# Cross attention in Strassen form: the fourth product moved in front of the next energy, and y's split ahead of gx's

## The chip, the cores and the metric

The kernel runs on one core of one Trainium2 chip. Its five engines work side by side: TensorE (PE) multiplies matrices into eight PSUM banks, VectorE (DVE), ScalarE (ACT) and GpSimd (POOL) work element by element, and SyncE (SP) issues transfers. The kernel fixes the order of the instructions on each engine; between engines it orders them by semaphores. Time is in microseconds (us) of device time for one execution of the whole program, lower is better.

## The reference

`x` and `y` (ctx) have shape 32 x 256 x 1024 in float32: 32 batches, 256 channels, 1024 positions. For each batch:

```python
x_q = w_qk @ y            # transposed: N x C
x_k = w_qk @ x
x_v = w_v @ x + b_v
energy = x_q.T @ x_k                               # N x N, 1024 x 1024
attention = softmax(energy, axis=-1)               # rows
attention = attention / (1e-7 + attention.sum(axis=1))   # columns
x_r = x_v @ attention
out = x + relu(w_t @ (x - x_r) + b_t)
```

The weights are 256 x 256. The column sums need all rows of the softmax, so the second half of a batch can't start before the whole energy has been exponentiated.

## The kernel before, in words

**Algebra.** The two uses of w_qk are folded into one matrix G, so that energy = y.T (G x). w_t and w_v are folded too, so that the output is w_t x minus (w_t w_v x) times the attention. Three products of a batch are done by a 2 x 2 block scheme of Winograd's kind with seven block products P1 to P7 in place of eight: `Keys` (gx = G x, names `pg`), `Values` (u, names `pu`) and `Attention` (the output, names `po`). Each has three PSUM banks, `one`, `two` and `three`. `one` takes P1, then P6 is added, then P7, then P4; between these additions a copy is read out of it: P1 (`p1s`), P1+P6 (`w`), with P7 (`c22`), with P4 (`c21`). `two` takes P5 (`p5s`), then P3 (`c12`); `three` takes P2 (`c11`). So a product that goes into `one` has to wait until the value before it has been read. `Attention`'s P-products consist of one part on x (`xpart`) and four on the attention tiles (`epart`, tiles 0 to 3). All seven are float32 products of 128 x 512, two matmul instructions each.

**Energy.** gx and y are each split into three parts in a faster matmul type (`Split`, tiles `gf` and `yf`): the high part, the lower part, and a mixed part. `parts(i)` writes all three on ScalarE for half i of the channels (3 instructions); `lower(i)` adds the original to the lower part by an accumulating transfer that GpSimd issues; `mixed(i)` adds the finished lower part to the mixed part by another one, which can be issued only after `lower(i)` has landed. The energy of row block n (8 of them) and column half h is six matmuls: two on the high parts, two on the lower, two on the mixed ones, so that the sixth of a row block's first half is the first to need the mixed part of half 1. `gather` copies one sum on ScalarE (`es`) and adds the other on VectorE while taking the row minimum; `exp` is ScalarE, `share` adds the row to the column sums (`acc`) on VectorE.

**Order of a batch.** The order is written out by hand: the class `InOrder` chains every instruction of an engine behind the one before it. A batch goes: energy rows 0 to 7; then `Keys` and the first part of `Values` of the next batch while VectorE finishes the column sums (`columns`, `inverse`); then the attention (`Attention.run`). In `run`, VectorE scales the exponentials (`normal`, 16 instructions) and makes the sums t1 to t4 of attention blocks (`mix`, two instructions each). t3 is written over t1 and t4 over t2, so t3 must wait until P5 has read t1, and t4 until P6 has read t2. The last product of the attention, P4 (`end`, `before.end()`, 5 products), with its read-out `c21`, stands in the next batch's energy, behind row block 0.

**Other queues.** GpSimd issues the eight accumulating transfers of the split, then the small copy `behind` that reads t4 (so that the following does not run beside the mixes), then the sums of the value blocks (`factors`: two additions to `ut`, four to `us`), then three accumulating transfers (`xsteps`) for the sums of x. SP issues the loads of y (two batches ahead), the four stores of the output blocks, two loads for the sums of x (`summed`) and the load of x (`load(b + 1)`).

**Buffers.** The eight PSUM banks are handed out in turn. `us`, `yf`, `gf`, `acc` and the attention tiles `e` and `et` have one buffer each; the output temporaries `z` have two.

Of the kernel before, what the change touches and what calls it, by code (L numbers as in the profile page):

```python
# [12 lines left out]
ALU = mybir.AluOpType  # L13
# [4 lines left out]
def kernel(  # L18
# [25 lines left out]
    KC = C // P  # L44
# [3 lines left out]
    HT = NT // 2  # L48
# [29 lines left out]
    pe, dve, act, pool = (InOrder(g) for g in (nc.tensor, nc.vector, nc.scalar, nc.gpsimd))  # L78
# [6 lines left out]
    def load(b, pieces=1):  # L85
        to = xp.tile([P, KC, N], F32, tag="x", name=f"x_{b}")
        from_ = x[b].rearrange("(k p) n -> p k n", p=P)
        W = KC // pieces
        for j in range(pieces):
            nc.sync.dma_start(to[:, ts(j, W)], from_[:, ts(j, W)])  # L90
        loaded[b] = to
# [43 lines left out]
    behind = const.tile([P, 1], F32, name="behind")  # L135
# [70 lines left out]
    def temp(tag, name):  # L206
        return cp.tile([P, MB], F32, tag=tag, name=name)
# [8 lines left out]
    def summed(b):  # L216

        s = up.tile([P, 4, MB], F32, tag="xs", name=f"xs_{b}")
        t1, t3, t4, t2 = (s[:, j] for j in range(4))
        to = loaded[b]  # L220
        b11, b12 = to[:, 0, ts(0, MB)], to[:, 0, ts(1, MB)]
        b21, b22 = to[:, 1, ts(0, MB)], to[:, 1, ts(1, MB)]
        if b == 0:
            pool.tensor_tensor(t1, b11, b12, ALU.add)
            pool.tensor_tensor(t2, b22, t1, ALU.add)
            pool.tensor_tensor(t3, b12, b22, ALU.add)
            pool.tensor_tensor(t4, b21, t2, ALU.add)
            steps = []
        else:
            q = quarters(x[b])  # L230
            nc.sync.dma_start(s[:, :2], q[:, 0, 1:2, :].to_broadcast([P, 2, MB]))
            nc.sync.dma_start(s[:, 2:], q[:, 1])
            steps = [
                lambda: accumulate(s[:, :2], corners(x[b])),
                lambda: accumulate(s[:, 2:], s[:, 0:1].to_broadcast([P, 2, MB])),
                lambda: accumulate(t4, q[:, 1, 1]),
            ]
        return (b11, b21, b22, t4, t1, t2, t3), steps
# [211 lines left out]
    class Attention(Seven):  # L450
# [76 lines left out]
        def run(self, u, before=None, between=None):  # L527


            self.normal(0, 0)  # L530
            self.normal(1, 0)
            for j in range(HT // 2):
                self.normal(0, 1, j)
                self.mix(self.t1, self.b11, self.b12, ALU.add, j)
            if u:
                u.c22()
            self.normal(1, 1)
            self.mix(self.t2, self.t1, self.b22, ALU.subtract)
            self.epart(self.one, 1)
            self.p1s = self.biased(self.one, "p1s", bt[:, 0, :])  # L540
            if u:
                between.parts(1)
                between.lower(1)
                between.mixed(1)
            self.epart(self.three, 2)
            self.epart(self.two, 5)
            self.p5s = self.biased(self.two, "p5s", bt[:, 1, :])
            self.xpart(self.one, 6, True)
            if u:
                u.p4()  # L550
                u.c21()
                u.c11()
                u.c12()
            self.c11()
            self.put()
            self.xpart(self.two, 3, True)
            self.epart(self.two, 3, (0, 1) if u else (0,))
            self.epart(self.one, 6)
            self.w = self.biased(self.one, "w", nbt[:, 0, :])
            self.mix(self.t3, self.b12, self.b22, ALU.subtract)  # L560
            if before:
                before.combine(1, 1, before.p5s, before.p7s, ALU.subtract)
                before.put()
                before.c21()
            self.mix(self.t4, self.b21, self.t2, ALU.subtract)
            self.epart(self.two, 3, (2,) if u else (1, 2))
            if u:
                self.epart(self.two, 3, (3,))
                self.c12()

        def end(self):
            self.xpart(self.one, 4, True)
# [20 lines left out]
    def columns(b):  # L593

        dve.tensor_reduce(
            parts[:, :, 0],
            acc.rearrange("p (j r) -> p j r", r=G32),
            AX.X,
            ALU.add,
            apply_transpose=True,  # L600
        )
# [22 lines left out]
    q = Queries(0)  # L624
# [4 lines left out]
    g = Keys(0, xr)  # L629
# [26 lines left out]
    u = Values(0, xr)  # L656
# [10 lines left out]
    before = None  # L667
    for b in range(B):
        more = b + 1 < B
        rows = []  # L670

        for n in range(NT):
            now = Energy(b, n, q.to, g.split.to)
            rows.append(now)
            now.products(0)
            if n == 0:
                e = ep.tile([P, NT, N], F32, tag="e", name=f"e_{b}")
                acc = one.tile([P, N], F32, tag="acc", name=f"acc_{b}")
            now.gather(0)
            now.products(1)  # L680
            now.gather(1)
            if n == 0:
                if b == 0:
                    u.p4()
                    u.c21()
                    xsteps[1]()
                    xsteps[2]()
                elif more:
                    before.end()
                    before.c21()  # L690
                    load(b + 1)
                if before is not None:

                    pool.tensor_copy(behind, before.t4[:, HT - 1, :1])
                if more:
                    ur, usteps = u.factors()
                    for step in usteps:
                        step()
                if more and b > 0:
                    xn, xsteps = summed(b + 1)  # L700
            if n > 0:
                rows[n - 1].exp()
            if n > 1:
                rows[n - 2].share()
            if more and b > 0 and n in (2, 4, 6):
                xsteps[n // 2 - 1]()

        if more:
            q = Queries(b + 1)
            for i in range(KC):  # L710
                q.load(i, nc.sync.dma_start)
            g = Keys(b + 1, xn)
            g.p1()
            rows[-1].exp()
            rows[-2].share()
            g.p5()
            g.p2()
            g.c11()
            rows[-1].share()
            g.p6()  # L720
            columns(b)
            g.p3()
            g.c12()
            g.p7()
            g.c22()
            un = Values(b + 1, xn)
            un.p1()
            un.p5()
            un.p2()
            un.p6()  # L730
        else:
            before.xpart(before.one, 7, True)
            rows[-1].exp()
            rows[-2].share()
            before.epart(before.one, 7)
            ur, usteps = u.factors()
            now = Attention(b, xr, ur)
            now.begin()
            rows[-1].share()
            columns(b)  # L740
            for step in usteps:
                step()
            before.p7s = temp("w", "p7s")
            act.copy(before.p7s, before.one)
        rc = inverse(b)
        if more:
            q.parts(0)
            q.lower(0)
            un.p3()
            g.p4()  # L750
            g.c21()
            un.p7()
            for i in range(KC):
                g.split.parts(i)
                g.split.lower(i)
            q.mixed(0)
            for i in range(KC):
                g.split.mixed(i)

        if more:  # L760
            now = Attention(b, xr, ur)
            now.begin()
            now.run(un, between=q)
            if b + 2 < B:
                now.xpart(now.one, 7, True)
                now.epart(now.one, 7)
                now.c22()
                now.put()
            now.put()
            before = now  # L770
            xr, u = xn, un
        else:
            before.end()
            now.run(None, before)
            now.finish()
# [30 lines left out]
```

## Time and profile before

| what | value |
|---|---|
| median of 3 runs | 2247.34 us (2243.19 to 2255.17) |
| the profiled execution | 2252.05 us, span 2250.2 us |
| TensorE / VectorE / ScalarE / GpSimd busy | 95% / 83% / 52% / 30% |
| mean granted TensorE clock | 0.973 |
| from one energy's start to the next, typical batch | 69.1 us (1006.61 to 1075.68) |
| of that, from the energy's first matmul to its restart behind P4 | 11.3 us (1006.61 to 1017.91) |

An instruction's line shows the start, the length, the engine, the operation, the tiles written and read (out<-in) and, in brackets, how long the engine was idle before it and what ended that. `L73` is the line of the helper that records every instruction, so tiles are told apart by their names: `pe` energy, `pg` gx, `pu` u, `po` output, `yfr` and `gfr` the unsplit rows. A stage's line gives its borders, its length, the busy time of PE, PE's weight loads, DVE, ACT and POOL, the granted clock (1.00 is full speed), the busy share of the DMA engines and their GB/s. Matmuls overlap their neighbours a little, so distances between starts are safer than the lengths shown.

### The profile page before, as it was taken

To read this page: it belongs to the slowest core of one execution; us is meant where nothing else is said; L and a number is where in the kernel's file an instruction comes from. 1 tells how busy PE (TensorE), PEld (TensorE's weight loads), DVE (VectorE), ACT (ScalarE), POOL (GpSimd) and SP (SyncE) were. 2 spreads that over 40 slices of the span, in tenths; PEclk is the share of its full clock that TensorE was granted. 3 is DMA by queue.
4 is the path that set the end of the run, shared out by engine and by line. 5 is a ranking of instruction groups with operands and counts; after the bars stand their busy time and mean duration, and the time that the engine had idled before them with its cause. 6 is when DMAs were issued, how large, how long until landed. Compare 5 with 4: busy or idle time off the path is not lost.

```text
span 2250.2 us, 23462 instructions
## 1 busy us (share of the span) xinstructions
PE 2132.7 (95%) x7586; PEld 1316.0 (58%) x7586; DVE 1875.9 (83%) x3024; ACT 1180.5 (52%) x1802; POOL 667.0 (30%) x582
## 2 busy tenths in 40 slices
PE   6999999999999999999999999999999999999998
PEld 4566555665556665556655566655666555665554
DVE  1988889877898888898788988888887789888888
ACT  4564545654456545556544565454664445654552
POOL 2333332223322333322233223333132332223321
PEclk7999999999999999999999999999999999999999
DMA  8455765646656567666476565675664756556650
GB/s 201 94 128 130 173 150 122 149 113 159 156 120 150 121 147 168 151 125 143 115 164 150 123 144 120 155 168 132 137 138 117 173 134 137 139 122 161 159 98 28
DMA packets 108954, 310.33 MB, mean 138 GB/s; under 512 B 10785, under 2 KB 11553, under 8 KB 108833
## 3 DMA queue, kind: packets, MB, share of 16 engines
q0 software_dynamic: 58192, 174.87, 42.4%
q1 hardware_dynamic: 50496, 133.85, 17.7%
q8 instruction: 60, 0.98, 0.2%
q14 instruction: 62, 0.50, 0.1%
q10 hardware_dynamic: 144, 0.13, 0.0%
HBM read 124.78 MB, written 33.55 MB: 70 GB/s over the span
## 4 chain that ended last, share of the span: by engine, by line
PE 72%; DMA 10%; issue 7%; ACT 6%; DVE 5%; POOL 0%; DVEq 0%; ACTq 0%; POOLq 0%
PE pe L73 30%; PE po L73 30%; PE pu L73 8%; DMA yf<-yf 6%; PE pg L73 4%; DVE e L73 3%; DMA yf<-yfr 2%; ACT e L73 2%; DMA gf<-gfr 1%; ACT gf L73 1%; ACT ow L73 1%; ACT es L73 1%; ACT yf L73 1%; ACT gp5s L73 1%; DVE acc L73 0%
## 5 line engine op out<-in xcount | busy, mean ns | idle before, releaser
L73 PE MATMUL pe<-gf,yf 128*128 128x512 f32 x3072 | 770.5, 410 | 87.9 <-DMA yf<-yf 78.2
L73 PEld LDWEIGHTS pe<-gf,yf 128*128 128x128 f32 x3072 | 591.0, 193 | 250.4 <-issue 109.4
L73 ACT ACTIVATE es<-pe 128x512 f32<-128x512 f32 x512 | 303.9, 594 | 465.4 <-PE pe L73 465.3
L73 PE MATMUL po<-et,us 128*128 128x512 f32 x768 | 350.3, 597 | 1.2 <-DVE et L73 1.2
L73 DVE SCALAR_TENSOR_TENSOR e<-e,ri,rc 128x512 f32<-128x512 f32 x512 | 347.4, 746 | 1.1
L73 DVE SCALAR_TENSOR_TENSOR acc<-e,ri,acc 128x1024 f32<-128x1024 f32 x224 | 289.9, 1294 | 8.0
L73 ACT ACTIVATE e<-e,nm 128x1024 f32<-128x1024 f32 x256 | 292.7, 1143 | 6.7 <-DVE nm L73 3.8
L73 DVE CUSTOM_DVE_ANT_0 e<-pe,es,nm 128x512 f32<-128x512 f32 x256 | 192.3, 751 | 81.2 <-ACT es L73 49.4
L73 PEld LDWEIGHTS po<-et,us 128*128 128x128 f32 x768 | 143.2, 190 | 192.9 <-issue 154.1
L73 PE MATMUL po<-e,ut 128*128 128x512 f32 x512 | 225.0, 592 | 1.0 <-DVE e L73 1.0
L73 DVE CUSTOM_DVE_ANT_0 e<-pe,es 128x512 f32<-128x512 f32 x256 | 175.6, 686 | 48.2 <-ACT es L73 32.0
L73 DVE SCALAR_TENSOR_TENSOR z<-z,x 128x512 f32<-128x512 f32 x96 | 214.6, 2260 | 1.2
L73 POOL DMA_DIRECT2D yf<-yfr x64 | 65.5, 1023 | 451.6 <-ACT yf L73 451.6
L73 PEld LDWEIGHTS po<-e,ut 128*128 128x128 f32 x512 | 97.2, 190 | 123.8 <-issue 107.9
L73 POOL TENSOR_TENSOR ut<-ut,bu 128x1024 f32<-128x1024 f32 x64 | 160.0, 2666 | 0.0
L73 POOL DMA_DIRECT2D yf<-yf x64 | 66.2, 1034 | 316.4 <-issue 267.5
L73 DVE TENSOR_TENSOR et<-e 128x1024 f32<-128x1024 f32 x128 | 153.7, 1222 | 5.1 <-DVE e L73 0.9
L73 ACT ACTIVATE yf<-yf 128x1024 fp32r<-128x1024 f32 x128 | 128.3, 1049 | 2.0
L73 ACT ACTIVATE gf<-gf 128x1024 fp32r<-128x1024 f32 x128 | 128.2, 1049 | 2.0
L73 POOL DMA_DIRECT2D xs<-in_x_dram x62 | 66.3, 1070 | 205.4 <-DMA xs<-xs 129.4
L73 PE MATMUL po<-e,us 128*128 128x512 f32 x256 | 120.5, 592 | 0.0
L73 PE MATMUL po<-et,ut 128*128 128x512 f32 x256 | 119.5, 610 | 0.0
(106 smaller groups left out, 2614.7 us busy)
## 6 DMA issues: line engine op xcount, KB each, us to landing
yfr<-in_ctx_dram SPq DMA_DIRECT2D x64, 512.0 KB, 6.4
yf<-yfr POOLq DMA_DIRECT2D x64, 512.0 KB, 6.1
gf<-gfr POOLq DMA_DIRECT2D x64, 512.0 KB, 5.8
yf<-yf POOLq DMA_DIRECT2D x64, 512.0 KB, 8.0
gf<-gf POOLq DMA_DIRECT2D x64, 512.0 KB, 9.4
out_dram<-z SPq DMA_DIRECT2D x128, 256.0 KB, 2.4
x<-in_x_dram SPq DMA_DIRECT2D x31, 1024.0 KB, 6.7
xs<-in_x_dram SPq DMA_DIRECT2D x62, 512.0 KB, 4.9
```

The costliest lines, as they stand in the source:

```text
L73: self.last = getattr(self.engine, name)(*args, **kwargs)
```

## The change

- P4 and its read-out leave the energy. A new `close()` at the attention's end holds P7, the last tile of P3, c22, P4, c12 and c21, so the energy of the next batch runs through all its rows without another product in between. In `run`, P3's tiles stand as 0, (P6), 1 and 2, (P7), 3.
- The split of y is issued in front of that of gx on ScalarE and on GpSimd: y's two halves first, lower and mixed, then gx's. What stands behind P1's copy in `run` is now the second half of gx (`between`) in place of the second half of y.
- GpSimd's `behind` and the sums of the values (`factors`) are written at the end of the attention of the same batch, in place of row block 0 of the next energy.
- The mix t3 stands directly behind t2 on VectorE, in front of u's c11 and c12 and of the output's c11.
- gx's P5 and its copy stand in front of the last row's exp.

```diff
             if u:
-                between.parts(1)
-                between.lower(1)
-                between.mixed(1)
+                between()
@@ run
                 u.c21()
+                self.mix(self.t3, self.b12, self.b22, ALU.subtract)
                 u.c11()
                 u.c12()
             self.c11()
             self.put()
             self.xpart(self.two, 3, True)
-            self.epart(self.two, 3, (0, 1) if u else (0,))
+            self.epart(self.two, 3, (0,))
             self.epart(self.one, 6)
             self.w = self.biased(self.one, "w", nbt[:, 0, :])
-            self.mix(self.t3, self.b12, self.b22, ALU.subtract)
             if before:
+                self.mix(self.t3, self.b12, self.b22, ALU.subtract)
...
             self.mix(self.t4, self.b21, self.t2, ALU.subtract)
-            self.epart(self.two, 3, (2,) if u else (1, 2))
-            if u:
-                self.epart(self.two, 3, (3,))
-                self.c12()
+            self.epart(self.two, 3, (1, 2))
+
+        def close(self):
+
+            self.xpart(self.one, 7, True)
+            self.epart(self.one, 7)
+            self.epart(self.two, 3, (3,))
+            self.c22()
+            self.put()
+            self.end()
+            self.c12()
+            self.put()
+            self.c21()
@@ energy, row block 0
                 elif more:
-                    before.end()
-                    before.c21()
                     load(b + 1)
-                if before is not None:
-
-                    pool.tensor_copy(behind, before.t4[:, HT - 1, :1])
-                if more:
+                if b == 0:
                     ur, usteps = u.factors()
                     for step in usteps:
                         step()
@@ behind the energy
             g.p1()
+            g.p5()
             rows[-1].exp()
             rows[-2].share()
-            g.p5()
...
             un.p7()
-            for i in range(KC):
-                g.split.parts(i)
-                g.split.lower(i)
+            q.parts(1)
+            q.lower(1)
             q.mixed(0)
-            for i in range(KC):
-                g.split.mixed(i)
+            g.split.parts(0)
+            q.mixed(1)
+            g.split.lower(0)
+
+            def between():
+                g.split.parts(1)
+                g.split.lower(1)
+                g.split.mixed(0)
+                g.split.mixed(1)
+
             now = Attention(b, xr, ur)
             now.begin()
-            now.run(un, between=q)
+            now.run(un, between=between)
+            pool.tensor_copy(behind, now.t4[:, HT - 1, :1])
             if b + 2 < B:
-                now.xpart(now.one, 7, True)
-                now.epart(now.one, 7)
-                now.c22()
+                now.close()
+                ur, usteps = un.factors()
+                for step in usteps:
+                    step()
+            else:
+                now.epart(now.two, 3, (3,))
+                now.c12()
                 now.put()
-            now.put()
```

## The prediction

> **What bounds the kernel now.** I read the page first, then the chain and the waits, then TensorE, GpSimd and VectorE in order of time in one typical batch (about 1006 us).
>
> From the page:
>
> ```profile
> span 2250.2 us, 23462 instructions
> PE 2132.7 (95%) x7586; PEld 1316.0 (58%) x7586; DVE 1875.9 (83%) x3024; ACT 1180.5 (52%) x1802; POOL 667.0 (30%) x582
> ```
>
> TensorE fills the span; VectorE, at 83%, is second. So the time is TensorE's work plus the places where it stops or runs slowly. The waits (total us, times, longest):
>
> ```profile
> PE pe L73 <- DMA yf<-yf: 78.2, 31, 3.7
> DVE z L73 <- ACT z L73: 103.6, 30, 5.1
> PE pg L73 <- ACT gp5s L73: 10.1, 31, 1.8
> PEld po L73 <- DVE et L73: 31.4, 63, 1.4
> ```
>
> TensorE has one wait of weight: once a batch, 2.5 us in the mean, for the transfer that forms y's third part. TensorE there, in order of time:
>
> ```profile
> 1003.58 3.60 PE L73 MATMUL po<-et,us 128*128 128x512 f32 x8
> 1006.61 1.72 PE L73 MATMUL pe<-gf,yf 128*128 128x512 f32 x5
> 1010.61 2.34 PE L73 MATMUL pe<-gf,yf 128*128 128x512 f32 x7 [2.27 <-DMA yf<-yf]
> 1012.75 1.91 PE L73 MATMUL po<-xs,wtT 128*128 128x512 f32 x2
> 1014.45 4.02 PE L73 MATMUL po<-et,ut 128*128 128x512 f32 x8
> 1017.91 19.63 PE L73 MATMUL pe<-gf,yf 128*128 128x512 f32 x84
> ```
>
> P7 ends, row 0 of the energy starts, its sixth matmul waits, then come seven matmuls, P4 (the two po lines) and the other 84 energy matmuls. The lines after the wait are slow: P4 takes 5.16 us (1012.75 to 1017.91), where the five equal products of P7 take 4.30 (1002.72 to about 1007.02). The stages say why (PEclk is the third figure from the end):
>
> ```profile
> 1010.60:1018.30 7.70, 7.69 (x18) 4.05 (x18) 4.71 (x6) 0.60 (x1) 6.75 (x5) 0.78 0.46 145
> 1018.30:1037.40 19.10, 19.10 (x86) 15.79 (x85) 14.94 (x35) 14.79 (x27) 3.33 (x3) 1.00 0.63 151
> ```
>
> A second price is thus paid after the wait, in granted clock. I read the two marks, first energy matmul and restart behind P4, in all 30 batches that have both. From restart to the next start it is 57.7 to 58.1 us nearly everywhere. From start to restart it is 9.09 to 13.88, mean 11.17. All that varies, and all that is lost, lies in that second stretch. Its work is 12 matmuls of 0.227 (82 take 18.61 in the chain) = 2.73, and P4's 4.30: 7.03. So 4.14 us a batch are lost, 2.5 to the wait and 1.6 to the clock.
>
> Why the transfer is late, GpSimd in order of time:
>
> ```profile
> 980.70 0.87 POOL L73 DMA_DIRECT2D yf<-yfr  x1 [12.73 <-ACT yf L73]
> 993.99 0.86 POOL L73 DMA_DIRECT2D gf<-gf  x1 [3.61 <-DMA gf<-gfr]
> 994.52 1.20 POOL L73 DMA_DIRECT2D yf<-yfr  x1
> 1006.01 0.86 POOL L73 DMA_DIRECT2D yf<-yf  x1 [10.28 <-issue]
> 1006.69 5.01 POOL L73 TENSOR_TENSOR ut<-ut,bu 128x1024 f32<-128x1024 f32 x2
> ```
>
> Eight accumulating transfers (two tensors, two halves, lower and mixed) go through one queue. With the issue-to-landing times of the DMA view, seven land at 985.9, 989.3, 993.5, 997.2, 1000.1, 1002.6 and 1005.5: 3.3 us apart in the mean, 2.5 to 4.2. The eighth, y's last, can be issued only when the seventh has landed (1006.01), with nothing else in the queue, and lands at 1010.6.
>
> **The change, part by part.**
>
> *P4 in front of the energy, per batch.* Five products of 0.86 move from behind row 0 to in front of it: no work is added. The same place in the new order, counted from this batch: P6 starts one product earlier, P7 ends at 1006.16, the last P3 product at 1007.02, P4 at 1011.3 plus a new wait. The new wait: P4 writes the bank that c22 reads on VectorE. The last batch already has this order at its end:
>
> ```profile
> 2240.74 1.02 PE L73 MATMUL po<-e,us 128*128 128x512 f32 x2
> 2241.68 1.13 PE L73 MATMUL po<-xs,wtT 128*128 128x512 f32 x2
> ```
>
> One P3 product (0.86) covers c22 (0.69, from 2240.94); P4 starts 0.08 late and its first product takes 0.11 longer. I take 0.2; ends 0.1 and 0.6 (0.54 is the longest wait of its kind on VectorE in that stretch). The energy starts at 1011.5.
>
> *y's forms ahead of gx's.* New GpSimd order: y lower 0 and 1, y mixed 0 and 1, then gx the same way. ScalarE's last three forms stay in the slot behind P1's copy, only now they are gx's. No transfer stands alone at the end now, since a mixed half has another half between it and its lower one. Eight landings, 3.3 apart from 985.9, end at 1008.9. The first matmul that needs the last one is the energy's sixth, at 1011.5 + 5 x 0.227 = 1012.6. Margin 3.7 us, so the wait goes to nothing. Bounds by the spacing rows: at 2.5 the last lands at 1003.4, at 4.2 at 1015.3, 2.7 late. I take the mean, since it is the same queue, with the same two y loads beside it.
>
> *The clock.* Half-speed stretches stand behind these waits; waits of 0.27 us (gx's P6 on its copy) have none behind them, the stage at 1018 to 1075 reads 1.00. So I take the 1.6 as gone; ends 0 and 1.6. The Trainium skill says otherwise: TensorE: Matmul & The Clock Gate, section "HAM oscillation — how this bites in real kernels", gives the rule that only idle gaps above about 3.4 us cost clock. By it a gap of 2.27 would not, and the 1.6 would stay, 2174 in all; the 0.78 above speaks against the rule.
>
> *GpSimd's sums at the attention's end.* Two adds to ut and four to us, 10.8 us (1006.69 to 1017.51), now start behind t4 (VectorE ends it at 1003.9), not behind y's last DMA: 1004.2 to 1015.0. They hold VectorE's adds of two SBUF tiles: a z add takes 0.69 alone, and with the first two sums beside it
>
> ```profile
> 998.72 0.69 DVE L73 SCALAR_TENSOR_TENSOR z<-z,x 128x512 f32<-128x512 f32 x1
> 1007.82 6.12 DVE L73 SCALAR_TENSOR_TENSOR z<-z,x 128x512 f32<-128x512 f32 x2
> 1019.23 0.69 DVE L73 TENSOR_TENSOR z<-z,x 128x512 f32<-128x512 f32 x1 [3.75 <-ACT z L73]
> ```
>
> that is, each is held until an idle moment of GpSimd. New: c22's put ends at 9.8 (ut's sums end 1009.2, and 0.55), c12's at 11.4, P4's z add, the third line above, is now held as well, to 1015.6. Behind it on VectorE stands the energy's first reduction, so at 4.1 us after the energy's start. TensorE needs that bank again with row 2, 28 x 0.227 = 6.4 after the start, so the reduction may start until 5.6. Rows 0 and 1 have no sum over rows, so VectorE catches up. Cost 0, cover 1.5 us; past that, each us costs 30 a run. The 3.75 wait for P4's z (103.6 in all) goes, worth nothing to TensorE. Next in GpSimd's queue is xs's first accumulate: at 1020.07 it waited 2.56 for TensorE, not for the sums, so it keeps its place behind the restart. P4's ScalarE pass now stands in front of row 0's first copy: it waits for P4 (1011.5) and for c22's store out of the same buffer (issued after 1009.8, 2.0 to 2.5 to land, so 1012.2) and ends at 1012.9; the copy, ready at 1012.6, is wanted by VectorE only at 1015.6. On SP, P4's store and the next x load follow the z add as before: x now about 2.1 us after the restart, 2.4 before. The two xs loads go in between the stores, no later.
>
> *Mix t3 behind t2* (2 x 1.2 us): it overwrites t1, which P5 has read by 993.3; t3 now starts at 996.8. The adds it passes (u's c11, c12, the output's c11 and put) come 2.35 later and feed only stores, bank releases and the sums, which start behind t4 anyway; t4 still ends at 1003.9. Cost 0, hidden under P6; without the cover 2.35.
>
> *gx's P5 ahead of the last exp*: removes the 0.27 of TensorE (10.1 / 31). But VectorE's t1 comes just in time for P5 (the 31.4 of weight loads on et, 0.5 each), so TensorE would only wait there. I take 0; ends 0 and -8 us in all. The exp comes 0.5 later; VectorE reads its sum 2 us after it.
>
> *The sum.* Per batch 11.17 - (2.73 + 4.30 + 0.2) = 3.94 saved, x 30 = 118. The last energy (no P4) waits 3.48 now; its last transfer comes some 3 us sooner: 3. Together 121. The profiled execution took 2252.05 (span 2250.2), 4.7 above the median 2247.34 of the three runs; the difference goes on the median: 2247 - 121 = 2126.
>
> **The rivals.**
>
> *The clock stays low* for another reason than the wait: 30 x 1.6 come back, 2174. For it: some batches with a 1.9 us wait show no loss, so the tie is not exact. Against: every stretch without the wait runs at 1.00.
>
> *VectorE late.* If the held z adds end 1 to 2 us past the cover, or c22's wait costs its upper end, 12 to 60 come back: 2138 to 2186. For it: single z adds took up to 5.7 us. Against: sums now start before the adds, so less of them is left to wait for.
>
> *The forms are later still, and it is slower.* Place: the energy's sixth matmul, now waiting for gx's last transfer, with the half clock behind it. The stretch is 7.23 + W + 1.6 and equals 11.17 at W = 2.3, a landing at 1014.9, a spacing of 4.1. At 4.6, the time of a transfer alone (1006.01 to 1010.6), it lands at 1018.1, W = 5.5: 30 x 3.2 = 95 more, about 2342. For it: one spacing of 4.2. Against: six had a mean of 3.3.
>
> *No change in effect*: the wait only changes its tensor and costs the same; 2236 to 2258 (0.5% is what a measurement of this kernel can tell). It needs a landing at 1014.7 to 1015.2, a narrow window.
>
> **How the numbers follow.** Forecast 0.70 (2106 to 2140: the gx wait's 8, and 12 for scatter, below; c22's upper end above), clock 0.07, VectorE 0.13, no change 0.04, slower 0.06. The first three are faster: 0.90, 0.04, 0.06. The range from 2106 to 2186 takes in the first three, less some tails.
>
> **What would show it.** Right: no TensorE wait for yf or gf of over 0.3 us past the first batch; granted clock near 0.99 over the run; start to restart gone, 64.7 to 65 us from energy to energy; y's last transfer before gx's first. Wrong: "PE pe <- DMA gf<-gf" at about 2 us a batch; VectorE's first reduction over 5.6 us after the energy's start with TensorE waiting for it; half clock behind the c22 wait.

## The result, and the profile after

The changed kernel takes 2131.1 us (median of 4, 2130.4 to 2133.0) against 2247.6 before: 0.948 of it, interval 0.9453 to 0.9506. The profiled execution has a span of 2128.9 us and a mean granted clock of 0.994 (before 0.973). The forecast was 2126, range 2106 to 2186.

From the page of the changed kernel:

```profile
span 2128.9 us, 23494 instructions
PE 2087.1 (98%) x7586; PEld 1290.6 (61%) x7586; DVE 1812.7 (85%) x3024; ACT 1179.7 (55%) x1802; POOL 681.3 (32%) x582
```

TensorE's 7586 instructions are as many as before, but their busy time is 46 us less: no work went, they no longer run at half clock. The rest of the 121 us of span is waiting. From its waits (total us, times, longest):

```profile
DVE z L73 <- ACT z L73: 51.2, 30, 2.5
PEld po L73 <- DVE et L73: 45.0, 62, 1.4
PE po L73 <- DVE et L73: 11.5, 33, 0.5
PE pe L73 <- DMA gf<-gf: 10.9, 3, 5.4
```

The line of 78.2 us for y's transfer is gone. What is left on a transfer is three waits, two of them in the first batch and one of 0.93 at the last energy. One line has grown from 1.2 us to 11.5: TensorE waits for VectorE's `et`, now once a batch. TensorE from P7 into the next energy, in order of time:

```profile
954.63 3.60 PE L73 MATMUL po<-et,us 128*128 128x512 f32 x8
958.07 1.02 PE L73 MATMUL po<-e,us 128*128 128x512 f32 x2
959.07 1.12 PE L73 MATMUL po<-xs,wtT 128*128 128x512 f32 x2
960.03 3.60 PE L73 MATMUL po<-et,ut 128*128 128x512 f32 x8
963.06 20.33 PE L73 MATMUL pe<-gf,yf 128*128 128x512 f32 x87
```

The first line is P7, the second the last P3 product, then P4 and the energy in one piece. P4 starts 0.14 late (959.07, not 958.93) and its first product takes 0.10 longer: that is the wait for c22, 0.24 in all. From one energy's start to the next it is 65.0 us from the third energy up to the last but one.

GpSimd in the same batch:

```profile
932.15 0.87 POOL L73 DMA_DIRECT2D yf<-yfr  x1 [15.38 <-ACT yf L73]
941.37 0.86 POOL L73 DMA_DIRECT2D yf<-yf  x1 [2.97 <-ACT gf L73]
951.71 0.86 POOL L73 DMA_DIRECT2D gf<-gf  x1 [7.72 <-DMA gf<-gfr]
954.46 0.86 POOL L73 DMA_DIRECT2D gf<-gf  x1 [1.89 <-DMA gf<-gfr]
956.07 4.66 POOL L73 TENSOR_TENSOR ut<-ut,bu 128x1024 f32<-128x1024 f32 x2
```

The last form is issued at 954.46 and lands 5.3 later, at 959.8; the matmul that needs it comes at about 964.6. Over 30 batches it lands 4.2 us ahead in the mean. VectorE, where the sums on GpSimd hold its adds:

```profile
959.04 2.23 DVE L73 SCALAR_TENSOR_TENSOR z<-z,x 128x512 f32<-128x512 f32 x1
961.91 1.04 DVE L73 SCALAR_TENSOR_TENSOR z<-z,x 128x512 f32<-128x512 f32 x1
964.68 1.21 DVE L73 TENSOR_TENSOR z<-z,x 128x512 f32<-128x512 f32 x1 [1.72 <-ACT z L73]
965.81 0.68 DVE L73 CUSTOM_DVE_ANT_0 e<-pe,es 128x512 f32<-128x512 f32 x1
```

All three z adds are held (0.69 alone), and the energy's first reduction starts at 965.81, 2.3 us after the energy's start (963.5, when P4's last product is out).

### The profile page after: what moved, and what is told of

Same layout as the page of the kernel before. It is cut to its first block, busy times and chain, and to the rows that moved or that the text cites. A ratio compares the mean times of both kernels' runs of the same rounds, so it can differ in the third digit from the quotient of the medians.

```text
span 2128.9 us, 23494 instructions
## 1 busy us (share of the span) xinstructions
PE 2087.1 (98%) x7586; PEld 1290.6 (61%) x7586; DVE 1812.7 (85%) x3024; ACT 1179.7 (55%) x1802; POOL 681.3 (32%) x582
## 4 chain that ended last, share of the span: by engine, by line
PE 61%; DVE 29%; issue 4%; ACT 1%; DMA 1%; DVEq 0%; POOL 0%; ACTq 0%; POOLq 0%
PE pe L73 31%; PE po L73 28%; DVE e L73 14%; DVE acc L73 4%; DVE et L73 4%; DVE gfr L73 3%; DVE rc L73 2%; DVE sc L73 1%; PE pu L73 1%; DVE parts L73 1%; ACT es L73 1%; DVE ri L73 0%; DMA gf<-gfr 0%; PE pg L73 0%; DMA gf<-gf 0%
## 5 line engine op out<-in xcount | busy, mean ns | idle before, releaser
L73 PE MATMUL pe<-gf,yf 128*128 128x512 f32 x3072 | 718.7, 394 | 10.9 <-DMA gf<-gf 10.9
L73 PEld LDWEIGHTS pe<-gf,yf 128*128 128x128 f32 x3072 | 578.0, 188 | 145.7 <-issue 27.3
L73 PE MATMUL po<-et,us 128*128 128x512 f32 x768 | 353.9, 597 | 11.5 <-DVE et L73 11.5
L73 POOL DMA_DIRECT2D yf<-yfr x64 | 55.0, 860 | 533.0 <-ACT yf L73 518.6
L73 ACT ACTIVATE z<-po,bt 128x512 f32<-128x512 f32 x31 | 21.4, 689 | 337.1 <-DMA out_dram<-z 234.5
L73 POOL TENSOR_TENSOR ut<-ut,bu 128x1024 f32<-128x1024 f32 x64 | 153.5, 2473 | 0.0
L73 POOL DMA_DIRECT2D gf<-gf x64 | 54.8, 856 | 306.3 <-DMA gf<-gfr 262.8
L73 DVE SCALAR_TENSOR_TENSOR z<-z,x 128x512 f32<-128x512 f32 x96 | 132.2, 1377 | 3.3
L73 PE MATMUL po<-e,us 128*128 128x512 f32 x256 | 125.3, 592 | 0.0
L73 POOL DMA_DIRECT2D xs<-xs x31 | 37.2, 1201 | 248.4 <-DMA xs<-in_x_dram 240.9
```

The lines of the kernel that those rows point to most:

```text
L73: self.last = getattr(self.engine, name)(*args, **kwargs)
```

## Experiments

All kernels start from the changed one unless it is said otherwise; `...` in an edit stands for lines left out. "Energy to energy" is the time from one energy's first matmul to the next one's. The runs were spread over several chips, on which the median of the kernel before was 2243.6 to 2248.6 us.

### One part at a time

**The split in its old order, P4 in front.** (Several calls are put on one line here, and the loops written out.)

```diff
-            q.parts(1); q.lower(1); q.mixed(0); g.split.parts(0); q.mixed(1); g.split.lower(0)
-            def between(): g.split.parts(1); g.split.lower(1); g.split.mixed(0); g.split.mixed(1)
+            g.split.parts(0); g.split.lower(0); g.split.parts(1); g.split.lower(1)
+            q.mixed(0); g.split.mixed(0); g.split.mixed(1)
+            def between(): q.parts(1); q.lower(1); q.mixed(1)
```

> The changed kernel with the split written in the old order (gx's halves in front, y's second half last); P4 stays in front of the energy. My theory: in the profile of before y's last transfer lands at 1010.6, and with P4 in front the energy's sixth matmul, the first that needs it, comes at 1012.6, so the wait is gone without the new order as well: 2131 us (2123 to 2140), granted clock 0.99. Rival, the order of the split is what removes the wait: then 1 to 2.5 us of wait a batch stay, and the half clock with them, 2131 + 30 x (2.6 to 4.1) = 2209 to 2254.

Measured: 2138.4 us (2137.9 to 2139.1), clock 0.992, 65.0 us from energy to energy in most batches. The waits show one place only where y's transfer still stops TensorE:

```profile
PE pe L73 <- DMA yf<-yf: 3.3, 1, 3.3
```

It is the last energy, which has no P4 in front, with 6.8 us at half clock behind it; 3.3 less 0.93, and 3.4 of clock, make 5.8 of the 7 us by which this kernel is behind the changed one. So with P4 in front the old order of the split has no wait either, up to the last energy. The small parts, gx's P5 and t3, are still in this kernel.

**P4 behind row 0 again, the split in its new order.**

```diff
@@ close
             self.put()
-            self.end()
             self.c12()
             self.put()
-            self.c21()
@@ energy, row 0
                 elif more:
+                    before.end()
+                    before.c21()
                     load(b + 1)
```

> The changed kernel with P4 and its read-out behind row 0 of the energy again; the new order of the split stays. The energy then starts 4.5 us sooner. From the profile after: the last transfer lands at 959.7 and the energy starts at 963.5, so it would land 0.7 after the new start, 0.4 ahead of the sixth matmul: no wait, c22's wait of 0.1 is covered too, 2127 us (2122 to 2137). By the estimate in the prediction (1008.9 against 1008.1) 0.8 of wait stay: 2155, and with the half clock 2203. Rival, P4's place is what matters and the order is worth nothing: near 2247.

Measured: 2138.1 us (2135.9 to 2139.6), clock 0.994. Between the two expected cases: past the first energy 18 of 31 sixth matmuls wait under 0.3 or not at all, the others up to 1.3, and past the start of the run there is nowhere a half clock. TensorE in the worst batch:

```profile
1025.15 1.71 PE L73 MATMUL pe<-gf,yf 128*128 128x512 f32 x5
1028.19 1.86 PE L73 MATMUL pe<-gf,yf 128*128 128x512 f32 x7 [1.33 <-DMA gf<-gf]
1029.89 1.02 PE L73 MATMUL po<-xs,wtT 128*128 128x512 f32 x2
1030.75 3.60 PE L73 MATMUL po<-et,ut 128*128 128x512 f32 x8
```

P4's part on x (two matmuls) takes 0.86 from start to start here (1.70 behind the 2.27 wait of before): full clock. So the new order of the split without P4's place, again with the small parts, brings nearly everything too. The two main parts are not added up: each removes the same wait.

**Both back.**

Both edits above in one kernel.

> The changed kernel with both the old order of the split and P4 behind row 0 again: what is left of the change is t3's place, gx's P5 in front of the exp, P3's tiles and c22 in front of c12. My theory: these are worth nothing, and the wait of before is back in full: 2247 us (2238 to 2255), granted clock 0.97. Rival, a part of the gain is theirs: below 2238.

Measured: 2196.6 us (2192.4 to 2199.3), clock 0.991. My theory fell: 51 us of the gain remain without the two main parts. Its wait, and that of the two kernels that follow:

```profile
PE pe L73 <- DMA yf<-yf: 53.0, 31, 3.0
```

53.0 where before had 78.2. In this kernel the first form is issued 26.36 us ahead of the energy (mean of 30 batches), in before 25.90; and y's last form lands 29.64 after the first one's issue, in before 30.00. Together 0.8 us less wait a batch, 25 us a run. The rest, as much again or a little more, is the clock: past the start 7 half-clock stretches of 3.4 us in place of 18 of 3.4 and 5 of 6.8, since most waits are now shorter than 1.8. Two kernels look for the causes, each with one more part undone.

gx's P5 behind the last exp as well:

```diff
@@ in the kernel with both back
             g.p1()
-            g.p5()
             rows[-1].exp()
             rows[-2].share()
+            g.p5()
             g.p2()
```

> The kernel with both main parts back (2196.6 us) and gx's P5 behind the last exp again as well. There the first form starts 26.36 us ahead of the energy in the mean, in before 25.90. My new theory: the forms hang on TensorE's u products, which come 0.27 sooner without gx's wait, while the energy's start hangs on VectorE's t1, so the early P5 gives the forms 0.46 us; taken back, the wait goes from 1.7 to about 2.2 and more batches go to half clock: 2225 us (2210 to 2240). Rival, the whole difference to before is t3's: 2197.

Measured: 2218.2 us (2211.0 to 2229.3). The first form is back at 25.88 us ahead of the energy, and the wait is 0.43 a batch longer:

```profile
PE pe L73 <- DMA yf<-yf: 66.4, 31, 3.4
```

t3 in its old place as well:

```diff
@@ in the kernel with both back
                 u.c21()
-                self.mix(self.t3, self.b12, self.b22, ALU.subtract)
                 u.c11()
...
             self.w = self.biased(self.one, "w", nbt[:, 0, :])
+            self.mix(self.t3, self.b12, self.b22, ALU.subtract)
             if before:
-                self.mix(self.t3, self.b12, self.b22, ALU.subtract)
                 before.combine(1, 1, before.p5s, before.p7s, ALU.subtract)
```

> The kernel with both main parts back (2196.6 us) and t3 in its old place as well. New theory: behind t2, t3 sends the first store of the output 2.35 us later, so that it no longer runs beside the seventh form (2.92 between the sixth and seventh landing in before, 2.48 there); with t3 back the wait grows by about 0.4: 2220 us (2205 to 2235). Rival, the whole difference is gx's P5: 2197.

Measured: 2204.2 us (2196.3 to 2216.9), just under the range expected:

```profile
PE pe L73 <- DMA yf<-yf: 59.1, 31, 3.1
```

The wait is 0.2 longer; the seventh landing comes 0.2 later (24.76 after the first issue, not 24.54), half of what was expected. The times of this kernel overlap with those of the one with both back, so the wait shows t3's effect, the time alone does not. gx's P5 is the larger one. By the medians the two make 22 and 8 of the 51 us. What the rest hangs on is open: no run has both undone at once, and none has P3's tiles or c22 and c12 in their old order.

**The sums of the values.** With them written at row 0 of the energy again, the program has the same instructions in the same order on all five engines, with the same waits. This part of the change moves nothing: GpSimd's queue has `behind` and the sums directly behind the last form in either text. They start sooner in the changed kernel because the last form is issued sooner.

**gx's P5 and t3, in the changed kernel itself.**

```diff
@@ first kernel: gx's P5
-            g.p5()
             rows[-1].exp()
             rows[-2].share()
+            g.p5()
@@ second kernel: t3
                 u.c21()
-                self.mix(self.t3, self.b12, self.b22, ALU.subtract)
...
             self.w = self.biased(self.one, "w", nbt[:, 0, :])
+            self.mix(self.t3, self.b12, self.b22, ALU.subtract)
             if before:
-                self.mix(self.t3, self.b12, self.b22, ALU.subtract)
```

> The changed kernel with gx's P5 and its copy behind the last row's exp again. My theory: VectorE's t1 sets when the output's P5 goes on, so the 0.27 us at gx's P6 comes back and the 0.33 at the output's P5 falls to about 0.06: 2131 us (2128 to 2134), 65.03 us from energy to energy as now. Rival, TensorE alone sets it: 31 x 0.27 = 8 more, 2139.

Measured: 2130.6 us (2129.6 to 2132.7), 65.0 us from energy to energy. TensorE waits 0.27 at gx's P6 again, and the 0.33 at the output's P5 has gone altogether.

> The changed kernel with t3 in its old place behind the output's c11, so TensorE gets t3 2.35 us later, u's c11 and c12 come 2.35 earlier. In the profile after t3 ends at 951.1 and P7 reads it from 954.6: late it would end at 953.5 and still be in time. No change, 2131 us (2128 to 2134). Rival, the adds in between are held by GpSimd's sums or P7 comes in front of t3: 10 or more slower.

Measured: 2131.1 us (2130.8 to 2131.6). Both are worth nothing where no transfer is waited for.

### What bounds the changed kernel

> The changed kernel with P6's part on x (0.86 us, needs nothing from VectorE) in front of the output's P5. My theory: the 0.33 us that TensorE waits for t1 at P5 are covered, 30 x 0.33 = 10 less; P3 now follows P5's copy with only u's P4 (0.89) between, which may cost 0.1 a batch: 2121 us (2119 to 2126), 64.7 us from energy to energy. Rival, VectorE is late by as much at the next place (t2 for P6): no change, 2131.

```diff
             self.epart(self.three, 2)
+            self.xpart(self.one, 6, True)
             self.epart(self.two, 5)
             self.p5s = self.biased(self.two, "p5s", bt[:, 1, :])
-            self.xpart(self.one, 6, True)
```

Measured: 2116.8 us (2115.7 to 2117.4), 0.9428 of before (0.9393 to 0.9463) where the changed kernel has 0.948: 14 us faster than it, though the two were not run side by side on one chip. 64.6 us from energy to energy. TensorE at P5 of the changed kernel:

```profile
941.11 1.88 PE L73 MATMUL po<-et,us 128*128 128x512 f32 x4
943.34 1.98 PE L73 MATMUL po<-et,us 128*128 128x512 f32 x4 [0.34 <-DVE et L73]
945.16 1.02 PE L73 MATMUL po<-xs,wtTs 128*128 128x512 f32 x2
```

and of this one:

```profile
933.84 1.02 PE L73 MATMUL po<-xs,wtTs 128*128 128x512 f32 x2
934.70 3.60 PE L73 MATMUL po<-et,us 128*128 128x512 f32 x8
938.13 1.05 PE L73 MATMUL pu<-wvtT,xs 128*128 128x128 f32 x8
939.08 1.12 PE L73 MATMUL po<-x,wtTs 128*128 128x512 f32 x2
```

P5 now runs through. The stop cost more than the 0.34 that the row names: from P5's start to the next product 4.05 there, 3.43 here, 0.62 less, of which P3's wait for P5's copy takes back about 0.15.

### How late VectorE may be at the energy's start

Idle VectorE passes behind P4's z add; they only repeat values. Three in the first kernel, seven in the second.

```diff
             self.put()
             self.c21()
+            two = self.t3[:, ts(0, 2)]
+            for _ in range(3):
+                dve.tensor_scalar(two, two, 1.0, None, ALU.mult)
```

> The changed kernel with three idle VectorE passes (1024 elements a partition, about 0.8 us each; they only repeat values) between P4's z add and the energy's first reduction: the reduction then starts about 4.7 us after the energy's start in place of 2.3. The prediction's figure for the cover says that it may start until 5.6: no change, 2131 us (2127 to 2137). Rival, VectorE sets the time since TensorE already waits 0.33 for it at P5, and every delay counts at once: 30 x 2.4 = 72 more, 2203.

> The same with seven such passes, about 5.5 us: the reduction starts 7.8 us after the energy's start, 2.2 past the cover. By the prediction each us past it costs 30 a run: 2131 + 66 = 2197 (2180 to 2230), with TensorE waiting for VectorE in rows 2 to 4. Rival 1, VectorE makes it up in its idle time of rows 0 to 3: 2131 to 2145. Rival 2, every delay counts: 2131 + 165 = 2296.

Measured: 2161.4 us (2159.9 to 2161.8), 1.0 a batch more; and 2249.7 us (2247.7 to 2252.7), 3.95 a batch more. VectorE of the first, and of the second:

```profile
978.71 3.34 DVE L73 TENSOR_SCALAR et<-et 128x1024 f32<-128x1024 f32 x3
981.97 0.67 DVE L73 CUSTOM_DVE_ANT_0 e<-pe,es 128x512 f32<-128x512 f32 x1
```

```profile
1017.25 6.25 DVE L73 TENSOR_SCALAR et<-et 128x1024 f32<-128x1024 f32 x7
1023.41 0.68 DVE L73 CUSTOM_DVE_ANT_0 e<-pe,es 128x512 f32<-128x512 f32 x1
```

In the mean the first reduction starts 5.66 and 8.56 after the energy's start (P4's last product out), in the changed kernel 2.6. So from 5.66 on, 2.90 more cost 2.94: each us counts in full, as predicted; but 5.66 costs 1.0 already, so the cover ends at about 4.65, not 5.6. What limits it is shown by VectorE's idle time between the first reduction and the column sums: 3.78 us in the changed kernel, 1.94 and 1.97 in these two. Only 1.84 of it is made up. The energy's bank is not what runs out first. With three passes TensorE never waits for VectorE in the energies past the first; its new wait comes behind them, for ScalarE's copy of gx. With seven it waits at the bank as well, 1.0 a batch of the 3.95 (TensorE's waits of the first kernel, then of the second, then its rows in the batch above):

```profile
PE pg L73 <- ACT gw L73: 14.4, 31, 1.0
```

```profile
PE pe L73 <- DVE nm L73: 29.2, 30, 1.7
```

```profile
1014.35 8.74 PE L73 MATMUL pe<-gf,yf 128*128 128x512 f32 x36
1024.16 10.05 PE L73 MATMUL pe<-gf,yf 128*128 128x512 f32 x42 [1.07 <-DVE nm L73]
```

The matmul that waits is the energy's 37th, in all 30 batches, so the bank is wanted 36 x 0.227 = 8.2 us after the start and not after 28 matmuls (6.4), as the prediction had it.

### The half clock

Small idle VectorE passes between P7 and c22, five or twelve, so that P4 waits longer.

```diff
             self.epart(self.two, 3, (3,))
+            for _ in range(5):
+                dve.tensor_scalar(few, self.one[:, :P], 1.0, None, ALU.mult)
             self.c22()
```

> The changed kernel with five small VectorE passes (128 elements a partition, about 0.2 us each) between P7 and c22, so that c22, and with it P4, comes about 1 us later. The wait is then about 1 us a batch: 30 more, 2161 us (2153 to 2175). The clock stays at 1.00, since waits of up to 1.4 us in the run with P4 behind row 0 had no half clock behind them.

> The same with twelve passes, about 2.4 us, the length of the wait of before, but ended by VectorE and not by a transfer. If the half clock follows the length of TensorE's wait: 30 x (2.4 + 1.6) = 120 more, 2251 us (2230 to 2265), granted clock 0.97 to 0.98. If it belonged to the transfers, or only to waits above 3.4 us as the Trainium skill has it (TensorE: Matmul & The Clock Gate, section HAM oscillation): 72 more, 2203, clock 0.99.

The passes took 0.29 us each, not 0.2, so the waits were 1.42 and 3.7. Measured: 2174.9 us (2174.6 to 2175.0), 30 x 1.46 more, clock 1.00 behind the wait; and 2329.2 us (2325.9 to 2330.7), clock 0.953, 6.65 a batch more: 3.7 of wait (4.72 from the last P3 product to P4 in place of 1.00) and 2.9 of clock (P4 takes 6.85 in place of 3.99). P4 behind the short wait, and behind the long one, then the stage of the latter (PEclk is the third figure from the end):

```profile
1179.34 1.12 PE L73 MATMUL po<-xs,wtT 128*128 128x512 f32 x2 [1.42 <-DVE z L73]
1180.30 3.60 PE L73 MATMUL po<-et,ut 128*128 128x512 f32 x8
```

```profile
1260.00 2.07 PE L73 MATMUL po<-xs,wtT 128*128 128x512 f32 x2 [3.70 <-DVE z L73]
1261.86 5.62 PE L73 MATMUL po<-et,ut 128*128 128x512 f32 x8
```

```profile
1260.00:1266.90 6.90, 6.90 (x10) 2.90 (x11) 2.47 (x3) 0.00 (x0) 4.77 (x4) 0.57 0.57 178
```

No transfer ends this wait, and the clock halves all the same: it follows the stop, not what ends it. This run can't decide between the half clock's price after 2.4 us and the rule of 3.4, since its wait came out at 3.7; the waits of the other runs do. In before, and in the kernel with both parts back, the granted clock in the trace halves for 3.4 us behind 15 of 22 waits for y's last form of 1.78 to 2.66 us and behind 7 of 13 of 1.8 to 2.97. Below that, none of the 17 such waits of 1.05 to 1.74 us in the kernel with both back, and none of the 30 of 1.42 here, has a half clock behind it.

## Why the prediction was right

**The bound.** Right: TensorE's wait for y's last form and the half clock behind it were the loss that the change went for. With the wait gone the clock is 1.00 in the middle of the run:

```profile
1018.00:1083.00 65.00, 64.67 (x238) 39.95 (x237) 56.63 (x95) 36.67 (x56) 21.69 (x19) 1.00 0.66 150
```

**P4 in front.** Right in mechanism and size: energy to energy 65.0 (predicted 64.7 to 65), c22's wait 0.24 (0.2). The last energy still waits 0.93 for gx's last form, above the 0.3 that the prediction gave as its sign.

**The forms.** Landing margin predicted 3.7 us, measured 4.2 in the mean. But the step did not ask what each of the two parts would do without the other. By its own numbers the answer was there: P4's place moves the sixth matmul to 1012.6, behind the 1010.6 of the old order, and the runs show 2138 with either part (and the small parts) in place. So the gain does not show that both were needed.

**The clock.** Right: the 1.6 a batch is gone, and the rival that it stays low for another reason fell: the clock halves behind a wait of 3.7 us that VectorE ends, and stays at 1.00 behind one of 1.42. The rule that I weighed (the Trainium skill, TensorE: Matmul & The Clock Gate, section "HAM oscillation — how this bites in real kernels": gaps above about 3.4 us) does not hold here, as 15 waits of 1.9 to 2.6 us in the kernel before cost it.

**The sums.** The verdict (nothing) was right, the reading was not: I took the change in the text for a move in GpSimd's queue, and there is none. On VectorE the lateness was mis-sized, 4.1 against 2.6 measured, and so was the cover, 5.6 against about 4.65: it is VectorE's idle time up to the column sums, not the bank, that gives it, and the bank itself is wanted 8.2 us after the start, not 6.4. Zero held all the same, as 2.6 lies well below 4.65; at the reckoned 4.1 about half a us of cover would have been left, not 1.5.

**t3 and gx's P5.** Zero in the changed kernel, as predicted, with TensorE waiting 0.33 for t1 in place of 0.27 for the copy. In a kernel that still waits for the forms the price of 0 does not hold: there gx's P5 is worth 22 us, and t3 about 8 by the medians, with ranges that overlap.

**The sum.** 121 us predicted on the profiled execution, 121.4 measured (2252.05 to 2130.66). Against the median 2247 it is 116, since that profile was one of the slower executions: here lies most of the 5 us between 2126 and 2131.

## What to carry to other kernels

When two edits each promise to remove the same wait, price each alone against the same deadline; here, beside the small parts, either brings 109 of the 116 us, and the second is mostly insurance. Where a stop of TensorE of about 2 us halves the clock it costs almost twice its length, so shortening a wait below 1.8 us already brings the clock's share. So small edits that are worth nothing without the wait made 51 us with it. When one wait is gone, look for the next: moving one product of 0.86 us that needs nothing from VectorE brought 14 us more.

## What the runs showed of the hardware that I had not expected

- Past the start of the run the half clock comes in pieces of 3.4 us, one or two of them. Behind waits of up to 1.74 us there was none; behind 3.7 us nearly always two (6.8 us).
- Whether a wait of 1.8 to 3 us halves the clock varies from batch to batch at the same length (2.34 us with and without). The clock records of the 14 traces show what decides: every change of the clock stands a whole number of 3.413 us steps behind the trace's first record, and TensorE's idle time inside one such step settles the next one. Past the first 80 us, of 8390 steps at full clock with less than 1.79 us of idle time none is followed by half clock, of 67 with 2.0 us or more all are, and of the 20 between them 9 are. So a wait of 2.97 us that a border cuts in two cost no clock (in the kernel with both back), and one of 1.91 us did (in before). The kernel with such waits also scatters more: 2211 to 2229 us with gx's P5 back, 2130.4 to 2133.0 in the changed kernel.
- A VectorE pass with one SBUF input takes longer beside GpSimd's sums as well: in the three-pass kernel all 30 passes that overlap with one took 1.77 to 1.78 us, the other 60 took 0.69 to 0.96.
